# A Mamba scan on VectorE: the product with C one unit late, its broadcast amid the unit, ScalarE's table visits behind the first decay

## The chip, the cores and the metric

The kernel runs on one core of a Trainium2 chip. The metric is the device time of one execution in microseconds, as the median of several runs. The profile is one execution taken by the hardware profiler. Its engines: PE is TensorE (PEld its weight loads), DVE is VectorE, ACT is ScalarE, POOL is GpSimd, SP is SyncE, which only issues DMAs here.

## What is computed

The reference is a hybrid block on an input of 4 x 1024 x 128 floats. Cut to what matters:

```python
x = x + attention(layernorm(x))     # sparse attention, 16 heads
x = x + ffn(layernorm(x))           # 128 -> 512 -> 512 -> 128 with +-1 weights
x = x + mamba(layernorm(x))
x = x + ffn(layernorm(x))           # the same FFN again
return x

# inside mamba: 256 channels e, 16 states n, one step for each time t
def step(h, inp):
    dt_t, B_t, C_t, u_t = inp
    dA = jnp.exp(dt_t[..., None] * A)                       # the decay
    h = dA * h + (dt_t * u_t)[..., None] * B_t[:, None, :]
    y_t = jnp.einsum('ben,bn->be', h, C_t)
    return (h, y_t)
# then y = (y + u * D) * silu(z), a projection back to 128, and the residual
```

## The kernel before, in words

The attention comes first, then set-up and the first FFN tiles; the change does not touch these. Then follows the scan stage (`scans`, called at line 1437), in which everything else still to do of both FFNs and of the Mamba layer is woven between the scans. Behind it stands a tail: whatever pieces of FFN work are left, and the last tiles.

**Units.** A part is one batch element b and one half f of the sequence (512 steps); there are 8 parts. A unit is one state n of one part, so there are 128 units (line 915). The 256 channels lie as two halves h of 128 partitions. For unit i:

- ScalarE makes the decays `da(i,0)` and `da(i,1)` by Exp into PSUM (`decay`, line 1178). There are only two PSUM buffers for them, so `da(i+1,0)` can be written only when the scan that reads `da(i,0)` is through.
- GpSimd makes the drive `db(i)` = du x B, two units ahead (`drive`, line 1151; three buffers).
- VectorE runs two scans over 512 steps, `hs(i,0)` and `hs(i,1)` (line 1263); `hs` has two buffers, so unit i+2 overwrites unit i.
- TensorE spreads C over the partitions in one matmul into the one PSUM buffer `pcc` (line 1257), and VectorE multiplies: `hc(i) = hs(i) * pcc` (line 1280). For the states n = 3, 8 and 13 (`BY_GP`) GpSimd does this product instead, from a C that a DMA has spread (`product_by_gp`, line 1170).
- GpSimd issues for every second unit a DMA that adds `hc(k)` to `hc(k+1)` (`gather`, line 1187), and TensorE sums the results over n in PSUM as `pys` (`add` and `total`, lines 1195 to 1214). At the end of a part VectorE multiplies by the gate (`gated`).
- For f = 0 ScalarE copies the last column of `hs` to `carry` (line 1271), from which the second half of the sequence starts.

**Order.** Inside the scan stage every engine executes in the order in which the program is written (`InOrder`, `keep`). Between a unit's own instructions `pieces(until)` (line 1333) issues work from a set of lists: norms, projections, convolutions, FFN tiles. A piece names how long it occupies which engine. The planner keeps its own clock of each engine in `times`, advanced by `spend`; a piece with TensorE work is issued only if it ends by `until` on that clock, and no engine gets more pieces than an allowance (`RATES`) that is refilled at each call. Evictions from PSUM (`evict=True`) go first. Some evictions are lumps: Silu and Softplus, which need another activation table than Exp, so that ScalarE loads a table, runs two activations and loads Exp's table again. `pieces(..., lumps=False)` does not issue those. Three PSUM banks (`SPARE`) are left for pieces. If a part's preparation isn't issued when a unit needs it, `ready` forces pieces out, at once and whatever they cost.

What is left in the lists after the last unit is issued by the loop at line 1440, still with three banks; then the last tile of the FFN follows with eight banks (line 1446).

Of the kernel before, what the change touches and what calls it, by code (L numbers as in the profile page):

```python
# [16 lines left out]
F32 = mybir.dt.float32  # L17
# [5 lines left out]
ALU = mybir.AluOpType  # L23
# [3 lines left out]
P = 128  # L27
# [10 lines left out]
E, N, DC, DR = 256, 16, 4, 8  # L38
NH = E // P
CH = 512  # L40
# [3 lines left out]
def hybrid_kernel(ctx: ExitStack, tc: tile.TileContext, x, Wq, Wk, Wv, Wo, ln_g, ln_b, W_in, conv_w,  # L44
# [17 lines left out]
    ve, te, sc, gp = (InOrder(e) for e in (nc.vector, nc.tensor, nc.scalar, nc.gpsimd))  # L62
# [19 lines left out]
    for bp in range(NP):  # L82
        t = xpool.tile([P, NT, C], F32, tag=f"x{bp}", name=f"x{bp}")
# [1050 lines left out]
    def scans(wide, ready):  # L1134

        bss, css, dbs, das, hss, hs_of = {}, {}, {}, {}, {}, {}
        BY_GP = (3, 8, 13)
        py = {}  # L1140
        last = len(units) - 1

        def load_b(i):

            if i <= last and i % 2 == 0:
                b, f, n = units[i]
                ready(b, f, "b")
                bss[i] = m2.tile([P, 2, CH], F32, name=f"bs{i}", tag="bs", bufs=2)
                nc.sync.dma_start(bss[i], mamba_pre[b, f][5][n : n + 2, :].partition_broadcast(P))

        def drive(i):
            if i <= last:
                b, f, n = units[i]
                ready(b, f, NH - 1)
                dbs[i] = m2.tile([P, NH, CH], F32, name=f"db{i}", tag="db", bufs=3)
                bs = bss[i - n % 2][:, n % 2]
                gp.tensor_tensor(dbs[i], mamba_pre[b, f][3], bs.unsqueeze(1).to_broadcast([P, NH, CH]), ALU.mult)

        def load_c(i):

            if i <= last and by_gp(i):
                b, f, n = units[i]
                ready(b, f, "b")
                css[i] = m1.tile([P, CH], F32, name=f"cs{i}", tag="cs")
                nc.sync.dma_start(css[i], mamba_pre[b, f][5][N + n, :].partition_broadcast(P))

        def by_gp(i):
            return units[i][2] in BY_GP

        def product_by_gp(i):  # L1170

            if i >= 0 and by_gp(i):
                gp.tensor_tensor(
                    hss[i], hs_of.pop(i), css.pop(i).unsqueeze(1).to_broadcast([P, NH, CH]), ALU.mult
                )
                done["hc", i] = spend("gp", 2.38, *after(("hs", i, 1)))

        def decay(i, h):
            if i <= last:
                b, f, n = units[i]  # L1180
                das[i, h] = wide.tile([P, CH], F32, name=f"da{i}_{h}", tag="da", bufs=2)
                sc.activation(das[i, h], mamba_pre[b, f][2][:, h], AF.Exp, scale=a_t[:, h, n : n + 1])

        def alone(k):
            return k > last - 2

        def gather(i):

            k = i - 2
            if k % 2 or not 0 <= k <= last or alone(k):  # L1190
                return False
            gp.dma_start(hss[k + 1], hss[k], accum_op=ALU.add)
            return True

        def add(k, h):

            b, f, n = units[k]
            first = (b, f, h) not in py
            if first:
                py[b, f, h] = wide.tile([P, CH], F32, name=f"pys{b}_{f}{h}", tag=f"pys{h}")  # L1200
                te.matmul(py[b, f, h], skip_d[:, h], mamba_pre[b, f][1][:, h], start=True, stop=False)
            te.matmul(py[b, f, h], ident, hss[k][:, h], start=False, stop=n == N - 1)
            return 2.0 if first else 1.0

        def total(i):

            us = 0.0
            h = i % 2
            k = i - 3 - h
            if 0 <= k <= last and not alone(k):  # L1210
                us += add(k, h)
            if alone(i - 1):
                us += sum(add(i - 1, h) for h in range(NH))
            return us

        def gated(i):

            h = 1 - i % 2
            k = i - 4 - h
            if 0 <= k <= last and units[k][2] == N - 1 and not alone(k):  # L1220
                gate_by(k, h)
                return True
            return False

        def gate_by(k, h):
            b, f, n = units[k]
            gate = mamba_pre[b, f][0]
            ve.tensor_mul(gate[:, h], gate[:, h], py.pop((b, f, h)))
            if h == NH - 1:
                fed.add(("g", b, f))  # L1230


        done = {}

        def after(*keys):
            return [done.get(k, 0.0) for k in keys]

        for i in range(3):
            load_b(i)
        for i in range(2):  # L1240
            drive(i)
            done["db", i] = spend("gp", 2.38)
        for h in range(NH):
            decay(0, h)
            done["da", 0, h] = spend("sc", 0.7)
        for i, (b, f, n) in enumerate(units):
            now[0] = i
            load_b(i + 3)
            product_by_gp(i - 1)
            load_c(i + 3)  # L1250
            drive(i + 2)
            done["db", i + 2] = spend("gp", 2.38, *after(("hs", i - 1, 1)))
            if gather(i):
                spend("gp", 0.9, *after(("hc", i - 1)))
            if not by_gp(i):
                pc = wide.tile([P, CH], F32, name=f"pcc{i}", tag="pcc")
                te.matmul(pc, spread[: 6 * N, n, :], mamba_pre[b, f][4], start=True, stop=True)
                done["pcc", i] = spend("pe", 0.4, *after(("pcc read",)))
            hs = m2.tile([P, NH, CH], F32, name=f"hs{i}", tag="hs")
            db = dbs.pop(i)  # L1260
            for h in range(NH):
                first = carry[b % 2][:, h, n : n + 1] if f else 0.0
                ve.tensor_tensor_scan(hs[:, h], das.pop((i, h)), db[:, h], first, ALU.mult, ALU.add)
                done["hs", i, h] = spend("ve", 1.235 if f else 1.175, *after(("da", i, h), ("db", i)))
            decay(i + 1, 0)
            done["da", i + 1, 0] = spend("sc", 0.67, *after(("hs", i, 0)))

            t = times["ve"]
            pieces(t + 2.5, lumps=False)
            if f == 0:  # L1270
                sc.copy(carry[b % 2][:, :, n : n + 1], hs[:, :, CH - 1 :])
            decay(i + 1, 1)
            done["da", i + 1, 1] = spend("sc", 0.67 if f else 0.86, *after(("hs", i, 1)))
            if gated(i):
                spend("ve", 0.68, *after(("sum", i - 1)))
            hss[i] = m2.tile([P, NH, CH], F32, name=f"hc{i}", tag="hc", bufs=6)
            if by_gp(i):
                hs_of[i] = hs
            else:
                ve.tensor_tensor(hss[i], hs, pc.unsqueeze(1).to_broadcast([P, NH, CH]), ALU.mult)  # L1280
                done["hc", i] = done["pcc read",] = spend("ve", 1.205, *after(("pcc", i)))
            done["sum", i] = spend("pe", total(i))
            t = times["ve"]
            pieces(t + 2.2)
        total(last + 1)
        for h in range(NH):
            gate_by(last, h)
# [6 lines left out]
    def spend(engine, us, *others):  # L1294
        times[engine] = max(times[engine], *others, 0.0) + us
        return times[engine]
# [36 lines left out]
    def pieces(until, lumps=True):  # L1333

        forced = not until
        evictions(lumps, forced)
        for k, rate in RATES.items():
            owed[k] = min(max(owed[k], -2 * rate) + (0 if forced else rate / 2), rate / 2)  # L1340
        left = SPARE - sum(w.held for w in works)

        for w in works[:-2] + sorted(works[-2:], key=lambda w: w.count):

            moved = w in emptied and now[0] < len(units) - 10
            while w.may() and not w.next.evict and w.next.banks <= left:
                if moved and not w.next.same and not (forced and w in emptied):
                    break
                if not (forced or w.next.hurries()):
                    if any(us and owed[k] <= 0 for k, us in w.next.us.items()):  # L1350
                        break
                    if "pe" in w.next.us and ends(w)[0]["pe"] > until:
                        break
                left -= w.next.banks
                issue(w)
                moved = True
            if forced and moved:
                break
# [121 lines left out]
```

## Time and profile before

| what | value |
|---|---|
| runs | 893.15, 897.59, 889.9 us; median 893.15 us |
| the profiled execution's own time | 896.53 us |
| its span, first to last instruction | 894.7 us, mean granted TensorE clock 0.912 |
| before the scan stage | 322.9 us |
| scan stage, first scan's start to last scan's end | 322.9 to 852.0 us: 529.1 us |
| tail behind the last scan | 42.6 us |
| busy in the scan stage | DVE 474.2, POOL 466.4, PE 458.6, ACT 405.5 us |

The page lists for each group of instructions its busy time and the mean duration of one, then the idle time of its engine just before them and what ended most of it. A line such as `A <- B` among the waits says that A's engine sat idle until B was done. All instructions that go through the ordering helper bear its line, L57, so the names of tiles tell them apart: `hs<-da,db` are scans of first halves, `hs<-da,carry,db` those of second halves.

### The profile page before, as it was taken

The page shows a single profiled execution, that of the slowest core. Times are in us where ns is not written, and L with a number is a line of the kernel's source. Part 1 is how long each engine was busy: PE and PEld are TensorE (multiplying, and loading weights), DVE is VectorE, ACT ScalarE, POOL GpSimd, SP SyncE. Part 2 cuts the span into 40 slices and gives each one's busy share as a digit, 9 for nine tenths or more (in the row PEclk, how much of TensorE's full clock was granted, in tenths as well). Part 3 has the DMA queues.
Part 4 walks back from the last instruction along what each step waited for, and adds up shares of the span by engine and source line. Part 5 has one row for each costly group of instructions (what it writes and reads, how often), then busy time and mean ns, then how long its engine had stood idle before and what let it go on. Part 6 is the DMA issues. An engine that isn't in the chain of part 4 may idle for free. (4 is left out here: it accounts for less than half of the span.)

```text
span 894.7 us, 16435 instructions
## 1 busy us (share of the span) xinstructions
PE 757.9 (85%) x6204; PEld 465.8 (52%) x6204; DVE 726.9 (81%) x970; ACT 606.3 (68%) x1358; POOL 682.5 (76%) x525
## 2 busy tenths in 40 slices
PE   5798878966788977788989788989889689889898
PEld 2455546645667653334546554535545345656567
DVE  6699998999563258898899998898988779999942
ACT  3776656754364488887878778878967766664523
POOL 6689966999342079999989998979979879877800
PEclk9899989997679989797999999899989799999999
DMA  4743133330010036564564656555565545666410
GB/s 127 129 74 73 27 57 68 74 70 2 3 48 1 1 109 155 127 159 129 137 148 130 153 130 153 145 121 138 155 154 133 141 112 150 164 145 153 108 25 19
DMA packets 59808, 92.77 MB, mean 104 GB/s; under 512 B 6200, under 2 KB 39776, under 8 KB 59728
## 3 DMA queue, kind: packets, MB, share of 16 engines
q1 hardware_dynamic: 49488, 58.15, 22.6%
q0 software_dynamic: 9680, 33.30, 19.8%
q8 instruction: 49, 0.80, 0.4%
q10 hardware_dynamic: 560, 0.26, 0.1%
q14 instruction: 31, 0.25, 0.1%
HBM read 52.11 MB, written 4.72 MB: 64 GB/s over the span
## 5 line engine op out<-in xcount | busy, mean ns | idle before, releaser
L57 POOL TENSOR_TENSOR db<-du,bs 128x1024 f32<-128x1024 f32 x128 | 315.6, 2504 | 23.8 <-DVE hs L57 20.1
L57 ACT ACTIVATE da<-dt,a_t 128x512 f32<-128x512 f32 x256 | 175.2, 687 | 107.1 <-DVE hs L57 106.8
L57 DVE TENSOR_TENSOR_SCAN hs<-da,db 128x512 f32<-128x512 f32 x128 | 149.9, 1209 | 29.7 <-ACT da L57 29.5
L57 DVE TENSOR_TENSOR_SCAN hs<-da,carry,db 128x512 f32<-128x512 f32 x128 | 156.7, 1266 | 5.5 <-ACT da L57 5.2
L57 PE MATMUL pys<-hc,ident 128*128 128x512 f32 x258 | 145.3, 649 | 1.9 <-DMA hc<-hc 1.8
L57 DVE TENSOR_TENSOR hc<-hs,pcc 128x1024 f32<-128x1024 f32 x104 | 126.7, 1218 | 22.1 <-PE pcc L57 15.9
L57 POOL TENSOR_TENSOR prodv<-vS,E 128x128 f32<-128x128 f32 (+14 forms) x30 | 69.6, 2319 | 12.2 <-ACT E L57 11.9
L57 PE MATMUL pga<-h1a,w 128*128 128x512 f32 x256 | 72.4, 435 | 5.1 <-ACT u L57 2.9
L57 PEld LDWEIGHTS pys<-hc,ident 128*128 128x128 f32 x258 | 49.6, 208 | 43.6 <-issue 37.2
L57 POOL TENSOR_TENSOR prod<-kv,qs 128x128 f32<-128x128 f32 (+14 forms) x30 | 71.3, 2376 | 1.0 <-DVE or L57 1.0
L57 POOL TENSOR_TENSOR hc<-hs,cs 128x1024 f32<-128x1024 f32 x24 | 58.1, 2421 | 13.6 <-DVE hs L57 11.6
L57 PE MATMUL pc<-mxnT,w_conv 128*128 128x512 f32 x128 | 63.3, 624 | 4.3 <-DVE h1b L57 2.4
L57 PEld LDWEIGHTS pga<-h1a,w 128*128 128x128 f32 x256 | 51.2, 201 | 27.4 <-issue 4.3
L57 POOL DMA_DIRECT2D hc<-hc x63 | 62.7, 995 | 1.8 <-issue 0.9
L57 ACT ACT_TABLE_LOAD x48 | 61.6, 1283 | 3.5 <-issue 2.6
L57 PE MATMUL pcc<-bc,spread 96*128 96x512 bf16 x104 | 42.0, 404 | 22.5 <-DVE hc L57 21.7
L57 ACT ACTIVATE E<-S 128x512 f32<-128x512 f32 (+15 forms) x62 | 26.5, 472 | 38.8 <-DVE S L57 38.6
L57 PE MATMUL ps<-kx,qT 64*32 64x256 f32 x1008 | 46.2, 432 | 6.3 <-DVE S L57 5.0
L57 POOL TENSOR_TENSOR du<-dt,u 128x512 f32<-128x512 f32 x16 | 24.8, 1551 | 29.7 <-ACT dt L57 29.6
L57 PEld LDWEIGHTS pc<-mxnT,w_conv 128*128 128x128 f32 x128 | 25.2, 199 | 37.4 <-issue 31.9
L57 ACT COPY ep<-pt 128x512 f32<-128x512 f32 x32 | 18.8, 587 | 36.4 <-DVE eo L57 36.1
L57 PE MATMUL pgb<-h1b,w 128*128 128x512 f32 x128 | 38.0, 447 | 1.4 <-ACT u L57 1.4
(245 smaller groups left out, 1682.9 us busy)
## 6 DMA issues: line engine op xcount, KB each, us to landing
bs<-bd SPq DMA_DIRECT2D x64, 512.0 KB
hc<-hc POOLq DMA_DIRECT2D x63, 512.0 KB, 4.6
vr<-vd SPq DMA_DIRECT2D x32, 256.0 KB
cs<-bd SPq DMA_DIRECT2D x24, 256.0 KB
vd<-kv SPq DMA_DIRECT2D x8, 256.0 KB
x<-in_L_attn_a_x_dram SPq DMA_DIRECT2D x15, 128.0 KB
kx<-kT SPq DMA_DIRECT2D x104, 16.0 KB
out_dram<-x SPq DMA_DIRECT2D x8, 128.0 KB
```

Source lines behind the costliest of these rows:

```text
L57: ins = getattr(self.engine, name)(*args, **kwargs)
```

## The change

For a unit i, VectorE's order was: scan(i,0), scan(i,1), pieces, gate if one is due, product(i), pieces. It becomes: scan(i,0), product(i-1), pieces, scan(i,1), gate, pieces. The matmul that spreads C for unit i moves from the head of unit i to behind product(i-1) and the first lot of pieces. The decay for (i+1,1) is issued directly behind scan(i,1), ahead of the copy to `carry`. The lumps go into the first lot, so that on ScalarE they stand between `da(i+1,0)` and `da(i+1,1)`; before, they stood between `da(i+1,1)` and `da(i+2,0)`. The DMA that gathers is issued behind product(i-1) of the same unit. The planner's limits change from 2.5 and 2.2 to 1.5 and 2.0 us, and its durations of a scan and a product are each some hundredths lower.

```diff
+        def product(i):
+            if i < 0 or by_gp(i):
+                return
+            hss[i] = m2.tile([P, NH, CH], F32, name=f"hc{i}", tag="hc", bufs=6)
+            ve.tensor_tensor(
+                hss[i], hs_of.pop(i), pcs.pop(i).unsqueeze(1).to_broadcast([P, NH, CH]), ALU.mult
+            )
+            done["hc", i] = done["pcc read",] = spend("ve", 1.15, *after(("pcc", i)))
+
         for i, (b, f, n) in enumerate(units):
...
             done["db", i + 2] = spend("gp", 2.38, *after(("hs", i - 1, 1)))
+            hs = hs_of[i] = m2.tile([P, NH, CH], F32, name=f"hs{i}", tag="hs")
+            db = dbs.pop(i)
+
+            def scan(h):
+                first = carry[b % 2][:, h, n : n + 1] if f else 0.0
+                ve.tensor_tensor_scan(hs[:, h], das.pop((i, h)), db[:, h], first, ALU.mult, ALU.add)
+                done["hs", i, h] = spend("ve", 1.21 if f else 1.15, *after(("da", i, h), ("db", i)))
+                decay(i + 1, h)
+
+            scan(0)
+            done["da", i + 1, 0] = spend("sc", 0.67, *after(("hs", i, 0)))
+            product(i - 1)
             if gather(i):
                 spend("gp", 0.9, *after(("hc", i - 1)))
+            t = times["ve"]
+            pieces(t + 1.5)
             if not by_gp(i):
-                pc = wide.tile([P, CH], F32, name=f"pcc{i}", tag="pcc")
-                te.matmul(pc, spread[: 6 * N, n, :], mamba_pre[b, f][4], start=True, stop=True)
+                pcs[i] = wide.tile([P, CH], F32, name=f"pcc{i}", tag="pcc")
+                te.matmul(pcs[i], spread[: 6 * N, n, :], mamba_pre[b, f][4], start=True, stop=True)
                 done["pcc", i] = spend("pe", 0.4, *after(("pcc read",)))
-            hs = m2.tile([P, NH, CH], F32, name=f"hs{i}", tag="hs")
-            db = dbs.pop(i)
-            for h in range(NH):
-                first = carry[b % 2][:, h, n : n + 1] if f else 0.0
-                ve.tensor_tensor_scan(hs[:, h], das.pop((i, h)), db[:, h], first, ALU.mult, ALU.add)
-                done["hs", i, h] = spend("ve", 1.235 if f else 1.175, *after(("da", i, h), ("db", i)))
-            decay(i + 1, 0)
-            done["da", i + 1, 0] = spend("sc", 0.67, *after(("hs", i, 0)))
-
-            t = times["ve"]
-            pieces(t + 2.5, lumps=False)
+            scan(1)
             if f == 0:
                 sc.copy(carry[b % 2][:, :, n : n + 1], hs[:, :, CH - 1 :])
-            decay(i + 1, 1)
             done["da", i + 1, 1] = spend("sc", 0.67 if f else 0.86, *after(("hs", i, 1)))
             if gated(i):
                 spend("ve", 0.68, *after(("sum", i - 1)))
-            hss[i] = m2.tile([P, NH, CH], F32, name=f"hc{i}", tag="hc", bufs=6)
             if by_gp(i):
-                hs_of[i] = hs
-            else:
-                ve.tensor_tensor(hss[i], hs, pc.unsqueeze(1).to_broadcast([P, NH, CH]), ALU.mult)
-                done["hc", i] = done["pcc read",] = spend("ve", 1.205, *after(("pcc", i)))
+                hss[i] = m2.tile([P, NH, CH], F32, name=f"hc{i}", tag="hc", bufs=6)
             done["sum", i] = spend("pe", total(i))
             t = times["ve"]
-            pieces(t + 2.2)
+            pieces(t + 2.0, lumps=False)
+        product(last)
         total(last + 1)
```

More of the change, by code (lines that the diff above doesn't have):

```diff
@@ L1134, in scans @@
     def scans(wide, ready):
-        bss, css, dbs, das, hss, hs_of = {}, {}, {}, {}, {}, {}
+        bss, css, dbs, das, hss, hs_of, pcs = {}, {}, {}, {}, {}, {}, {}
         BY_GP = (3, 8, 13)
```

## The prediction, made before the changed kernel had run

> **What bounds the kernel now.** I read the page first (shares, slices, groups), then VectorE's waits, then the timelines where they lie; last, since a planner places the pieces, the instruction order of both built programs.
>
> ```profile
> PE 757.9 (85%) x6204; PEld 465.8 (52%) x6204; DVE 726.9 (81%) x970; ACT 606.3 (68%) x1358; POOL 682.5 (76%) x525
> DVE  6699998999563258898899998898988779999942
> ```
> ```profile
> L57 DVE TENSOR_TENSOR_SCAN hs<-da,carry,db 128x512 f32<-128x512 f32 x128 | 156.7, 1266 | 5.5 <-ACT da L57 5.2
> L57 DVE TENSOR_TENSOR hc<-hs,pcc 128x1024 f32<-128x1024 f32 x104 | 126.7, 1218 | 22.1 <-PE pcc L57 15.9
> L57 ACT ACT_TABLE_LOAD x48 | 61.6, 1283 | 3.5 <-issue 2.6
> ```
> ```profile
> DVE hs L57 <- ACT da L57: 34.7, 26, 8.3
> DVE hc L57 <- PE pcc L57: 15.9, 11, 4.3
> ```
>
> In the scan stage (322.9 to 852.0 us, 529.1 us) VectorE is busy 474 us and is the bound: the slices read 8 and 9. It waits 47.9 us there: 26.3 for decays (34.7 less 8.3 before the first scan), 15.9 for spread C, 5.7 for evictions and a gate. So 481.2 us are its own pace. The waits for decays sit behind ScalarE's table visits; one of them:
>
> ```profile
> 618.90 0.69 ACT L57 ACTIVATE da<-dt,a_t 128x512 f32<-128x512 f32 x1
> 619.61 1.28 ACT L57 ACT_TABLE_LOAD   x1
> 620.90 1.27 ACT L57 ACTIVATE dt<-pd,bdt 128x512 f32<-128x512 f32 x2
> 622.19 1.28 ACT L57 ACT_TABLE_LOAD   x1
> 623.48 0.69 ACT L57 ACTIVATE da<-dt,a_t 128x512 f32<-128x512 f32 x1
> ```
> ```profile
> 618.86 1.22 DVE L57 TENSOR_TENSOR hc<-hs,pcc 128x1024 f32<-128x1024 f32 x1
> 620.00 2.33 DVE L57 TENSOR_TENSOR_SCAN hs<-da,db 128x512 f32<-128x512 f32 x2
> 624.27 2.34 DVE L57 TENSOR_TENSOR_SCAN hs<-da,db 128x512 f32<-128x512 f32 x2 [1.95 <-ACT da L57]
> ```
>
> From the scan that frees the first decay's buffer (ended about 618.8) to the scan that needs the second, ScalarE takes 5.4 us: two decays of 0.69, a visit of 3.9, hand-overs. VectorE has 3.6 us of work in that window, and waits the rest.
>
> **The change, part by part** (against the profiled execution: 896.53 us, span 894.7 and 1.8 around it, 3.4 above the median of 893.15).
>
> *The product leaves its own scan.* From start to start in VectorE's timeline a scan with a carry takes 1.19 us ahead of something that doesn't read it and 1.35 ahead of its own product; without a carry 1.13 and 1.29: 0.155 us for the dependence. By the order of before, 73 of 104 products stand straight behind their scan: 73 x 0.155 = -11.3 us. The Trainium skill (VectorE: DVE Perf Modes, The DRAIN you can't avoid) says that the next operation starts only once the pipe is empty, wait or no wait. That speaks against a gain; by it this term is 0 and the forecast 11.3 us longer. The starts above show one, and I take the row.
>
> *Table visits behind the first decay.* I put each of the 22 visits through the same sum: ScalarE's durations between the two decays, VectorE's between the two scans, from the instruction order. As a test on before: 19.6 us at visits and 5.9 elsewhere, 25.5 in all, where the trace has 26.3. For after, ScalarE needs 5.43 as before. VectorE's cover is product, scan, scan, product = 1.14 + 1.16 + 1.16 + 1.14 = 4.60 (before 4.91: two dependences more): 0.83 of wait, at 10 visits. Beside a GpSimd unit one product is missing: 3.46, so 1.97, at 5; with a gate in its place 4.04, so 1.39, at 3. Two are covered (0.17 and 0). At units 62 and 94 a Softplus visit is now forced out when the drive needs it, behind the second decay with only 2.33 and 2.92 us of cover: 4.88 and 2.70. Sum 8.3 + 9.9 + 4.2 + 0.2 + 7.6 = 30.1. Other ScalarE pieces ahead of a second decay beside a GpSimd unit (four normalizations, twice with two sums) give 1.27, 0.14, 1.88, 1.92, 0.43, 1.27, 0.35 = 7.3. So 37.4 for 26.3: +11.1. Bounds: 27 (as before) and 45 (the forced visits doubled). The same skill (ScalarE: Activation LUTs, What ACT_TABLE_LOAD costs) adds a drain of about 1.38 us to each load; above, the next activation starts 0.01 us after it. By the page each visit would be 2.8 us longer, in both versions.
>
> *GpSimd's products lose a product's length of cover.* With two scan buffers, unit i+2's first scan waits for GpSimd's product of unit i. Between them VectorE had two scans, a product, and often a dependence more; now the product lies one scan later, so 1.29 us (1.14 + 0.155) go. In the timelines of before, 7 of 24 such products end within 1.29 us of that scan, for example 0.04 us here (the scans start at 496.57):
>
> ```profile
> 494.17 2.36 POOL L57 TENSOR_TENSOR hc<-hs,cs 128x1024 f32<-128x1024 f32 x1
> ```
>
> Together they lack 7.1 us; some lie beside a visit's wait already, so +5, bounds 1 and 31 (all 24 of them 1.29). GpSimd's drives are hidden: they end 4 to 7 us before their scans.
>
> *Spread C, gather, pys.* The matmul goes behind up to 1.5 us of pieces, not 2.2, and the product asks for it one scan later than its bank is free, as before. TensorE also has less in the stage (below). 9 for 15.9: -6.9; bounds 4 and 20. The gather's DMA is held by the product one scan longer on GpSimd's queue, where the next drive stands behind it; those 4 to 7 us hide that. If a transfer (4.6 us to land) is late for pys, TensorE stalls and the next spread C with it; that is in the upper bound. SP's loads are not moved past anything. The carry copy behind the decay: 0, nothing ended on it.
>
> *Work left over.* With shorter limits fewer pieces fit. Behind the last pys TensorE has 205 matmuls in the order of before and 337 in that of after: the same ones, moved out. In before they ran between 797 and 855 us:
>
> ```profile
> L57 PE MATMUL pgc<-h1c,w 128*128 128x512 f32 x64 | 17.6, 418 | 0.7 <-DVE h1c L57 0.5 <-ACT h2c L57 0.2
> L57 PE MATMUL pfoc<-w,h2c 128*128 128x128 f32 x64 | 8.3, 278 | 0.0
> L57 PE MATMUL pfc<-fxnTc,w 128*128 128x512 f32 x8 | 3.0, 481 | 0.8 <-ACT h2c L57 0.8
> ```
>
> With pmo (2.7 + 1.7), the 256-wide pfc (2.6) and ftpc (1.2) that is 37.1 us. The tail has no room for it:
>
> ```profile
> 857.60:876.30 18.70, 17.44 (x136) 15.27 (x136) 4.68 (x17) 6.08 (x17) 1.26 (x2) 1.00 0.03 9
> 876.30:894.60 18.30, 13.94 (x117) 13.50 (x116) 4.95 (x13) 5.93 (x18) 0.00 (x0) 0.97 0.07 22
> ```
>
> TensorE is busy 17.4 of 18.7 us with three banks, and the last 18.3 us are the last tile's own chain, which waits for the FFN in front of it. So +37; bounds 28 (the 5.7 idle us filled and a clock of 1.00 instead of 0.92) and 45 (evictions with three banks exposed). VectorE's share of that work leaves the stage: six h1c, two ox, four statistics, two narrow fxnTc: -7.1.
>
> *Sum.* Stage: -11.3 + 11.1 + 5 - 6.9 - 7.1 = -9.2. Tail +37. Together +27.8: 924.3 against the profiled 896.5, and 921 against the median.
>
> **The rivals.**
>
> 1. *The visits hide after all.* The second decay's scan now stands behind a scan and two products; if ScalarE gets far enough ahead for that to cover a visit, waits on decays go to 0 instead of 37.4: 921 - 37.4 = 883.5, not slower. Against it: 5.43 of ScalarE does not fit in 4.60, and the same sum meets the trace of before within 1 us. It decides from about 10 us of such waits: below that the kernel gains, above it loses.
> 2. *The tail is cheap.* Moved matmuls fill its gaps (+28), and waits in the stage stay at 47.9 in all: 481.2 - 11.3 - 7.1 + 47.9 = 510.7, -18.4; 893.15 - 18.4 + 28 = 903. For it: TensorE is idle 5.7 us there, less work crowds the stage. Against it: the last 18.3 us wait for that work.
> 3. *GpSimd's products set the pace.* If all 24 come late, 31 instead of 5: 947. For it: POOL is busy 466 of 529 us. Against it: its drives stand 4 to 7 us ahead, and waits of VectorE give it time.
>
> **How the numbers follow.** Forecast 0.62 (912 to 936), rival 1 0.07 (876 to 896), rival 2 0.15 (897 to 911), rival 3 0.16 (936 to 955). The time is the forecast's, 921. The range 898 to 947 leaves out rival 1 and half of rival 3. A measurement here tells about 1% from no change: faster means under 884.2, slower over 902.1. Half of rival 1 is faster: 0.04. The other half and over half of rival 2 are the same: 0.12. The rest is slower: 0.84.
>
> **What would show it.** Right: scans end near 843 us and the tail is 75 to 85 us, TensorE nearly full in it; starts of scan and following product 1.13 to 1.19 apart; second scans (not first ones) of a unit wait for decays, 30 us or more in the stage, worst at units 62 and 94; little wait for spread C. Wrong: a stage under 490 us, waits on decays under 15, or a tail under 65.

## The result, and the profile after

The changed kernel takes 924.88 us (median of 4 runs, 923.36 to 926.06) for 891.74 us before, measured beside it: 1.036 times as long, 95% interval 1.031 to 1.041. The forecast was 921 us, with a range of 898 to 947. The profiled execution took 926.06 us, with a span of 924.2. The two profiles differ by 29.5 us, less than the medians (33.1), because the profiled execution of before, 896.53 us, lies above the median of before.

| part of the span, us | before | after | difference | forecast |
|---|---|---|---|---|
| ahead of the first scan (the same instructions) | 322.9 | 320.8 | -2.1 | 0 |
| scan stage | 529.1 | 523.9 | -5.2 | -9.2 |
| tail | 42.6 | 79.5 | +36.9 | +37 |
| VectorE in the stage: its own pace | 481.2 | 460.9 | -20.3 | -18.4 |
| waits for decays | 26.3 | 28.5 | +2.2 | +11.1 |
| waits for spread C | 15.9 | 17.5 | +1.6 | -6.9 |
| waits for GpSimd | 0 | 13.3 | +13.3 | +5 |
| other waits | 5.7 | 3.8 | -1.9 | 0 |

The stage became 5 us shorter and the tail 37 us longer. Of the waits for GpSimd, 11.6 us are for its products and 1.7 for one drive. From the page of the changed kernel, engines' shares and VectorE's slices:

```profile
PE 752.6 (81%) x6204; PEld 460.9 (50%) x6204; DVE 720.5 (78%) x970; ACT 608.5 (66%) x1358; POOL 683.9 (74%) x525
DVE  6699999999524288797898998788997988997222
```

The work is the same, instruction for instruction, and so are the busy times within 7 us; all shares are lower because the span is longer. VectorE's last three slices read 2 where before only the last one did: the tail is three slices now. The windows of the changed kernel show the stage, the tail with three PSUM banks, and the last tile (columns: stretch, its length, then busy us and instructions of PE, PEld, DVE, ACT, POOL, granted clock, DMA share, GB/s):

```profile
320.80:844.70 523.90, 425.31 (x1465) 229.70 (x1464) 460.50 (x447) 397.65 (x840) 466.28 (x335) 0.93 0.57 140
844.70:905.90 61.20, 56.43 (x328) 44.12 (x326) 15.06 (x41) 16.76 (x40) 2.97 (x6) 0.93 0.04 12
905.90:924.20 18.30, 13.93 (x116) 13.50 (x116) 4.90 (x13) 5.94 (x18) 0.00 (x0) 1.00 0.07 22
```

TensorE is busy 56.4 of 61.2 us in the tail, while VectorE and ScalarE have 15 and 17 us of work there. In the stage TensorE lost 33 us of work (458.6 to 425.3) and that by itself shortened nothing, since VectorE sets the stage's pace. The last tile is the same 18.3 us.

VectorE's waits in the changed kernel (us in all, times, longest):

```profile
DVE hs L57 <- ACT da L57: 28.5, 20, 5.0
DVE hc L57 <- PE pcc L57: 17.5, 13, 4.3
DVE hs L57 <- POOL hc L57: 11.6, 10, 4.1
DVE hs L57 <- POOL db L57: 1.7, 1, 1.7
```

The first two stood in the profile before with 26.3 us in the stage and 15.9; the waits for GpSimd are new.

### The profile page after: what moved, and what is told of

It is laid out like the page before. It is cut to its first block, busy times and chain, and to the rows that moved or that the text cites. A ratio compares the mean times of both kernels' runs of the same rounds, so it can differ in the third digit from the quotient of the medians.

```text
span 924.2 us, 16448 instructions
## 1 busy us (share of the span) xinstructions
PE 752.6 (81%) x6204; PEld 460.9 (50%) x6204; DVE 720.5 (78%) x970; ACT 608.5 (66%) x1358; POOL 683.9 (74%) x525
## 5 line engine op out<-in xcount | busy, mean ns | idle before, releaser
L57 POOL TENSOR_TENSOR db<-du,bs 128x1024 f32<-128x1024 f32 x128 | 318.9, 2540 | 17.7 <-DVE hs L57 10.8
L57 DVE TENSOR_TENSOR_SCAN hs<-da,carry,db 128x512 f32<-128x512 f32 x128 | 158.7, 1268 | 17.1 <-ACT da L57 11.4
L57 PE MATMUL pys<-hc,ident 128*128 128x512 f32 x258 | 147.9, 661 | 7.0 <-DMA hc<-hc 7.0
L57 DVE TENSOR_TENSOR hc<-hs,pcc 128x1024 f32<-128x1024 f32 x104 | 124.5, 1197 | 17.5 <-PE pcc L57 17.5
L57 PEld LDWEIGHTS pys<-hc,ident 128*128 128x128 f32 x258 | 51.7, 207 | 85.2 <-issue 55.2
L57 PE MATMUL pcc<-bc,spread 96*128 96x512 bf16 x104 | 42.6, 410 | 43.6 <-DVE hc L57 43.5
L57 POOL TENSOR_TENSOR prodv<-vS,E 128x128 f32<-128x128 f32 (+14 forms) x30 | 69.6, 2319 | 11.6 <-ACT E L57 11.4
L57 POOL TENSOR_TENSOR hc<-hs,cs 128x1024 f32<-128x1024 f32 x24 | 59.6, 2484 | 16.8 <-DVE hs L57 12.9
L57 PEld LDWEIGHTS pga<-h1a,w 128*128 128x128 f32 x256 | 50.4, 200 | 28.5 <-issue 5.3
L57 PE MATMUL pc<-mxnT,w_conv 128*128 128x512 f32 x128 | 59.5, 598 | 0.8 <-DVE h1b L57 0.8
L57 POOL TENSOR_TENSOR du<-dt,u 128x512 f32<-128x512 f32 x16 | 21.2, 1395 | 31.8 <-ACT dt L57 31.8
```

The costliest lines, as they stand in the source:

```text
L57: ins = getattr(self.engine, name)(*args, **kwargs)
```

## The experiments

The theory: the changed order and the planner's shorter limits together leave TensorE work over that the tail pays in full, while in the stage VectorE gains the time that it lost to the dependence (the product had to wait for its own scan) and gives as much back, 13.3 us, to a new wait for GpSimd. The rivals: the new order as such fills the stage, so that work put back would lengthen it as much; or the limits alone are to blame; or the place of the table visits. TensorE's matmuls behind the last pys are counted from the instruction order of each kernel; the traces show more records there (252 where the count is 205, 432 where it is 337).

**e1, the limits of before in the new order.**

```diff
-            pieces(t + 1.5)
+            pieces(t + 2.5)
...
-            pieces(t + 2.0, lumps=False)
+            pieces(t + 2.2, lumps=False)
```

> The changed kernel with the planner's two limits of before (2.5 and 2.2 us in place of 1.5 and 2.0), all else as changed. Behind the last pys TensorE has 257 matmuls (changed kernel 337, before 205). The two measured tails, 42.6 us at 205 and 79.5 at 337, give 0.28 us a matmul. Theory (the loss is FFN work left over for the tail): tail 57 us, 22 less; the stage takes back VectorE's share, some 4 us; about 907 us. Rival (the new order itself makes the stage full, and work put back lengthens it by as much): 922 to 927 us, with a stage of about 545 us for 523.9.

Measured: 913.17 us, 1.025 of before (1.020 to 1.029), between the two. The tail fell even further than the theory says, to 51.9 us, but the stage grew by 16.8 us to 540.7, nearer the rival's 545 than the theory's 528. VectorE's own pace rose by 6.1 us to 467.0, and its three main waits rose too:

```profile
DVE hs L57 <- ACT da L57: 32.4, 17, 16.6
DVE hc L57 <- PE pcc L57: 20.5, 16, 3.0
DVE hs L57 <- POOL hc L57: 16.6, 10, 3.5
```

A single wait for a decay stands out, in VectorE's timeline of this kernel:

```profile
572.63 3.63 DVE L57 TENSOR_TENSOR_SCAN hs<-da,carry,db 128x512 f32<-128x512 f32 x3
592.84 1.28 DVE L57 TENSOR_TENSOR_SCAN hs<-da,carry,db 128x512 f32<-128x512 f32 x1 [16.58 <-ACT da L57]
```

That is the first scan of unit 63. In unit 62 the next part's preparation had not been issued in time and was forced out between two decays; in the changed kernel the same scan waited 4.98 us. It waits 11.6 us longer here, but the other waits for decays became 7.7 us shorter, so this one wait doesn't explain the longer stage. Taken alone, e1 leaves the rival open.

**e2, limits and allowances both wider.** Limits 3.0 and 3.0, and:

```diff
-    RATES = {"pe": 2.9, "ve": 1.2, "sc": 2.4, "gp": 1.2}
+    RATES = {"pe": 3.2, "ve": 1.3, "sc": 2.6, "gp": 1.3}
```

> The changed kernel with both limits at 3.0 us and allowances raised from 2.9, 1.2, 2.4, 1.2 to 3.2, 1.3, 2.6, 1.3. 181 matmuls are left behind the last pys. Theory (left-over work): tail about 36 us, 43 less than the changed kernel's 79.5; stage longer by VectorE's share and some more waits for spread C, 8 us; about 890 us, level with before. Rival (the stage is full): about 922 to 927 us.

Measured: 892.84 us, 1.002 of before (0.999 to 1.005). Windows of this kernel:

```profile
318.80:854.30 535.50, 461.60 (x1671) 261.90 (x1670) 469.96 (x468) 407.61 (x866) 467.56 (x339) 0.91 0.55 138
854.30:892.30 38.00, 33.59 (x239) 28.19 (x237) 10.81 (x30) 10.97 (x32) 1.26 (x2) 0.95 0.07 19
```

TensorE has 461.6 us of work in the stage again, 36 more than in the changed kernel, and the stage is 11.6 us longer while the tail is 41.5 us shorter. So the stage was not full. The theory holds, and with it goes the whole loss: the new order, given enough pieces, is level with the kernel before. Whether the limits or the allowances did it was not separated. The stage itself gained nothing: it is 6.4 us longer than before, the tail 4.6 us shorter and the stretch ahead of the stage, with the same instructions, 4.1 us shorter.

**e3, the limits and planned durations alone, in the old order.**

```diff
-            pieces(t + 2.5, lumps=False)
+            pieces(t + 1.5, lumps=False)
...
-            pieces(t + 2.2)
+            pieces(t + 2.0)
```

and the planned durations 1.21, 1.15 and 1.15 of the changed kernel.

> The kernel before, in its own order, with the changed kernel's limits (1.5 and 2.0 us) and planned durations (scan 1.21 and 1.15, product 1.15). 223 matmuls are left behind the last pys, for 205. Theory (limits and order together leave the work over; limits alone do little): tail 5 us longer, stage up to 5 us shorter: 888 to 898 us. Rival (limits and durations alone make the loss): 915 us or more.

Measured: 891.23 us, 1.001 (0.998 to 1.004); tail 45.4 us. In the old order the limits do nothing. Matmuls left over: 205 before; 223 with the limits and planned durations alone, 257 with the order and those durations (e1), 337 with all. The two work on each other.

**e4, the table visits alone behind the first decay, in the old order.**

```diff
-            pieces(t + 2.5, lumps=False)
+            pieces(t + 2.5)
...
-            pieces(t + 2.2)
+            pieces(t + 2.2, lumps=False)
```

> The kernel before, with the table visits alone moved behind the first decay (lumps in the first lot of pieces, not in the second); product still straight after its own scan. Theory (what covers a visit is the work of VectorE between the two scans around it): in this order the cover is scan, product, scan = 3.6 us against 5.4 of ScalarE; the sum over all windows gives 51 us of waits for decays for 25.5 in before; 189 matmuls are left, so the tail is 4 us shorter: about 913 us. Rival (the place of the visits hardly matters, ScalarE catches up elsewhere): 886 to 896 us.

Measured: 909.35 us, 1.020 (1.015 to 1.024). VectorE's wait for decays in this kernel, the start of the stage (8.3 us) included:

```profile
DVE hs L57 <- ACT da L57: 50.0, 26, 8.3
```

41.7 us within the stage, for 26.3 before. The window sum had 51, so it was too high; the time is near the 913 expected, and the rival is out.

**e5, the visits alone put back behind the second decay, in the new order.** The same exchange, in the changed kernel.

> The changed kernel with the table visits back where they were (lumps in the second lot of pieces), all else as changed. 337 matmuls are left behind the last pys, as in the changed kernel. Theory (a visit is covered by what VectorE has between the two scans around it): behind the second decay the cover is now scan, product, scan = 3.5 us for 5.4; the window sum gives some 50 us of waits for decays where the changed kernel measured 28.5; tail the same: 938 to 946 us. Rival (the place of the visits doesn't matter): 922 to 927 us.

Measured: 936.19 us, 1.048 of before (1.044 to 1.052), where the changed kernel has 1.036. That is just under the theory's range and well over the rival's.

```profile
DVE hs L57 <- ACT da L57: 43.2, 21, 7.6
```

43.2 us for 28.5. So a visit's place and the product's place belong together: 26.3 (both old), 41.7 (visits moved alone), 43.2 (product moved alone), 28.5 (both moved; these last two with the shorter limits). The move of the visits doesn't lower the waits; it keeps the product's move from raising them.

**e6, three buffers for the scans' results.** In exchange the buffers that hold the products go from six to five, at all three places that name them; one is shown.

```diff
-            hs = hs_of[i] = m2.tile([P, NH, CH], F32, name=f"hs{i}", tag="hs")
+            hs = hs_of[i] = m2.tile([P, NH, CH], F32, name=f"hs{i}", tag="hs", bufs=3)
...
-            hss[i] = m2.tile([P, NH, CH], F32, name=f"hc{i}", tag="hc", bufs=6)
+            hss[i] = m2.tile([P, NH, CH], F32, name=f"hc{i}", tag="hc", bufs=5)
```

> The changed kernel with three buffers for the scans' results (hs) and five for the products (hc), for two and six; same order of instructions. Theory (the new wait for GpSimd's products, 11.6 us, is a wait for the scan buffer): it vanishes, the stage is 8 to 11 us shorter, the tail stays at 79 us: 914 to 917 us. Rival (VectorE then waits at the next thing, GpSimd's drives or decays): 921 to 926 us.

Measured: 920.61 us, 1.031 (1.027 to 1.034). The wait for GpSimd's products is gone, so it was a wait for the buffer; but the stage is only 3.2 us shorter (520.7). VectorE's waits in this kernel:

```profile
DVE hs L57 <- ACT da L57: 31.3, 21, 5.0
DVE hc L57 <- PE pcc L57: 17.6, 11, 3.9
DVE hs L57 <- POOL db L57: 3.5, 2, 1.8
```

Beside 11.6 us less there are 2.8 more for decays, 1.8 more for drives and 3.4 more for evictions and a gate, 8.0 in all. So the time comes nearer the rival's than the theory's: some 70% of the wait moved on.

**e7, e2 with the third buffer.**

> The changed kernel with limits of 3.0 us, allowances of 3.2, 1.3, 2.6, 1.3 and three scan buffers (five for products): both losses that the theory names undone. Against the same without the third buffer (892.8 us, waits for GpSimd's products 10.6 us): theory 882 to 885 us, 1% under before. Rival (the wait moves on): 890 to 894 us.

Measured: 886.23 us, 0.992 of before (0.989 to 0.996). The lowest median of the study, just above the theory's 882 to 885, and below that of both kernels. Its profiled execution, one of the faster ones (span 879.3), has a stage of 524.7 and a tail of 36.4 us. Here the buffer's wait did not move on:

```profile
DVE hc L57 <- PE pcc L57: 22.9, 19, 3.4
DVE hs L57 <- ACT da L57: 21.3, 22, 2.7
```

Waits for GpSimd are 2.8 us for 11.3 in e2, for decays 21.3 for 19.2, for spread C 22.9 for 24.6.

**e8, the allowances of e2 alone, in the old order.**

> The kernel before in its own order and limits, with the allowances alone raised to 3.2, 1.3, 2.6, 1.3. 189 matmuls are left behind the last pys, for 205. It says what the allowances give without the new order. Theory (the new order is worth its 11 us of dependence and pays for it with waits for GpSimd and for spread C): tail 4 us shorter, window sum of waits for decays 18.6 for 25.5: 880 to 887 us. Rival (the raised allowances only help the new order): 889 to 894 us.

Measured: 889.04 us, 0.995 (0.994 to 0.997): the rival's number more than the theory's. VectorE's waits in this kernel (8.3 us of the first are the start of the stage):

```profile
DVE hs L57 <- ACT da L57: 24.6, 23, 8.3
DVE hc L57 <- PE pcc L57: 15.2, 14, 2.6
DVE hs L57 <- POOL hc L57: 3.0, 3, 1.6
```

So it has waits for decays of 16.3 us for 26.3, but a tail of 44.0 us, no shorter than before. Against e2, with the same allowances and nearly the same work in the stage (468 instructions of VectorE in both), it shows what the order does, though e2's limits are wider as well: VectorE's own pace 482.6 us here, 471.1 in e2, so 11.5 us less; waits for spread C and GpSimd 19.0 here, 36.0 in e2. The order's gain is real and is eaten by these two: at like allowances the new order is the slower one (1.002 of before in e2, 0.995 here, and the intervals do not meet). Between e7 and e8 the intervals overlap, so which of them is the faster stays open, and no gain by the new order over the old one is shown.

**e9, the spread of C at the head, in the changed kernel.** The matmul goes ahead of the first lot of pieces.

```diff
-            t = times["ve"]
-            pieces(t + 1.5)
             if not by_gp(i):
...
+            t = times["ve"]
+            pieces(t + 1.5)
             scan(1)
```

> The changed kernel with the matmul that spreads C ahead of the first lot of pieces, straight behind the product that frees its bank, all else as changed. The planner then counts TensorE as taken up to the product's end before each first lot, and 493 matmuls are left behind the last pys (changed kernel 337). Theory (what is left over is paid for in the tail at 0.28 us a matmul): tail about 123 us; the window sum gives up to 60 us of waits for decays, for 28.5 measured; waits for spread C fall from 17.5 to under 10: 960 to 990 us. Rival (the tail is cheap beyond some point, since TensorE runs undisturbed there): 930 to 950 us.

Measured: 1025.26 us, 1.148 (1.144 to 1.152), well over both expectations. The tail is 110.9 us for 493 matmuls (0.24 us each over before's 205, not 0.28), and waits for spread C are 0.85 us, as expected. What neither theory had is the stage, 594.4 us, with 89.1 us of waits for decays within it and 37.5 of evictions that waited for FFN matmuls. VectorE's timeline of this kernel:

```profile
575.52 0.75 DVE L57 SCALAR_TENSOR_TENSOR x<-pfoa,total,x 128x512 f32<-128x512 f32 x1 [15.27 <-PE pfoa L57]
...
603.92 2.46 DVE L57 TENSOR_TENSOR_SCAN hs<-da,carry,db 128x512 f32<-128x512 f32 x2 [24.16 <-ACT da L57]
```

With so few pieces placed, the preparation of the parts at units 64 and 96 was forced out whole. The longest single wait, 36.5 us, stands at unit 94. So this run says little of the matmul's place by itself.

**e10, the spread at the head, in e7, with limits of 4.0.**

> The version of limits 3.0, raised allowances and three scan buffers (886.2 us, tail 36.4, waits for spread C 22.9 us), with the matmul that spreads C ahead of the first lot and limits of 4.0 us, so that 215 matmuls are left for 181. Theory (the matmul's wait is its place behind up to 3 us of pieces on TensorE's queue): waits for spread C fall to about 10, tail 9 us longer: 880 to 885 us. Rival (the product waits for TensorE wherever the matmul stands, since the bank is free only for two scans): 890 to 896 us.

Measured: 897.58 us, 1.006 (1.004 to 1.008): 12 us over the theory's range and even over the rival's. VectorE's waits in this kernel (8.3 us of the first are the start of the stage):

```profile
DVE hs L57 <- ACT da L57: 49.3, 36, 8.3
DVE hc L57 <- PE pcc L57: 5.0, 6, 1.8
```

The wait for spread C falls from 22.9 to 5.0 us: it does come from the matmul's place behind pieces on TensorE's queue, and there the theory's mechanism holds. The tail is 45.3 us, 9 more, as expected. But waits for decays rise from 21.3 to 41.0 within the stage, more than the 17.9 us that were saved. Whether that is the longer lots that a limit of 4.0 allows on ScalarE or the earlier matmul was not told apart.

## Why the prediction was right, point by point

*The work left over* carried it: +37 forecast, +36.9 measured. It was read without any time of the new kernel: the instruction order says which matmuls move behind the last pys, the trace of before what they took there. That it agrees to 0.1 us is luck: TensorE's busy time in the tail rose by 33.4 us (37.0 to 70.4), not 37.1, and its idle time by 3.5 (5.6 to 9.1), where the step left it as it was. All runs together, in order of the matmuls left over:

| matmuls left | tail, us |
|---|---|
| 181 | 38.1 (e2), 36.4 (e7) |
| 189 | 41.8 (e4), 44.0 (e8) |
| 205 | 42.6 (before) |
| 215 | 45.3 (e10) |
| 223 | 45.4 (e3) |
| 257 | 51.9 (e1) |
| 337 | 79.5 (changed kernel), 77.4 (e5), 79.2 (e6) |
| 493 | 110.9 (e9) |

The tail follows the count, at no fixed price: 0.18 us a matmul from 205 to 257, 0.35 from there to 337 and 0.20 from there to 493.

*The product leaves its own scan*: right in kind and size. VectorE's own pace fell by 20.3 us for 18.4 forecast (11.3 of dependence and 7.1 of moved work), and e2 against e8 gives 11.5 us for the order. Both differences also hold something that was not forecast: each of the 104 products became 0.026 us shorter (last section), some 2.7 us by our estimate. In the timeline of the changed kernel:

```profile
745.68 2.45 DVE L57 TENSOR_TENSOR_SCAN hs<-da,carry,db 128x512 f32<-128x512 f32 x2
748.05 1.19 DVE L57 TENSOR_TENSOR hc<-hs,pcc 128x1024 f32<-128x1024 f32 x1
749.16 2.45 DVE L57 TENSOR_TENSOR_SCAN hs<-da,carry,db 128x512 f32<-128x512 f32 x2
```

Two scans and a product go by in 3.48 us. In the timeline before, where the product follows its own scan:

```profile
771.47 2.45 DVE L57 TENSOR_TENSOR_SCAN hs<-da,carry,db 128x512 f32<-128x512 f32 x2
774.01 1.22 DVE L57 TENSOR_TENSOR hc<-hs,pcc 128x1024 f32<-128x1024 f32 x1
775.15 2.45 DVE L57 TENSOR_TENSOR_SCAN hs<-da,carry,db 128x512 f32<-128x512 f32 x2
```

it takes 3.68. The second scan of each pair starts 1.19 us behind the first and takes 1.26. In the changed kernel the product, which belongs to another unit, starts 1.18 us after that scan's start, 0.08 us before the profile has it end; before, the scan's own product started 1.35 us after it, 0.09 us behind its end.

The prediction weighed a rule of the Trainium skill (VectorE: DVE Perf Modes, The DRAIN you can't avoid), that the next operation starts only when the pipe is empty, whether or not it waits, and read from it a gain of 0. That reading was too narrow: the same section adds that a next operation that is not held starts earlier. The rows above show such a start, and the gain with it.

*Table visits*: the mechanism was right, the sum too large. Forecast 37.4 us of waits for decays, measured 28.5. At single visits the window sum is good: for the one forced out in unit 62, 4.88 forecast and 4.98 measured (at the first scan of unit 63); in 94, 2.70 and 2.70 (unit 95); at the second scans of units 7, 0.83 and 0.87, and 25, 1.97 and 1.99. Unit 62 on ScalarE in the changed kernel:

```profile
583.06 1.07 ACT L57 ACTIVATE h2a<-pga 128x512 f32<-128x512 f32 x2
584.14 1.28 ACT L57 ACT_TABLE_LOAD   x1
585.44 1.27 ACT L57 ACTIVATE dt<-pd,bdt 128x512 f32<-128x512 f32 x2
586.72 1.28 ACT L57 ACT_TABLE_LOAD   x1
588.02 1.30 ACT L57 ACTIVATE da<-dt,a_t 128x512 f32<-128x512 f32 x2
```

and on VectorE, the wait that it makes:

```profile
580.21 3.62 DVE L57 TENSOR_TENSOR_SCAN hs<-da,carry,db 128x512 f32<-128x512 f32 x3
588.81 1.28 DVE L57 TENSOR_TENSOR_SCAN hs<-da,carry,db 128x512 f32<-128x512 f32 x1 [4.98 <-ACT da L57]
```

The 22 visits made 23.1 us for 30.1 forecast, other places 5.4 for 7.3. What failed is adding the terms up. At units 15, 28, 58 and 107 the sum had 5.6 us of wait for decays and there is none, because in the same windows VectorE already waited 4.1 us for GpSimd, 4.3, 1.7 and 1.9 for spread C. In these four windows the two waits did not add up. The other 3.3 us of the 8.9 were not traced to a place.

*Spread C*: wrong in sign. Forecast 9, measured 17.5. The step held that less TensorE work in the stage and a shorter lot ahead of the matmul would bring it earlier. In the middle it does: half of these matmuls start within 0.80 us of the bank coming free, for 1.18 before, and TensorE waits longer for the bank, 43.5 us for 21.7. But VectorE waits only for the late ones, 13 of them for 11 before, and these are no earlier than then. (Two scans, some 2.4 us, pass between the bank coming free and the next product, in both orders, not one as the step has it.) The longest, 4.30 us, from TensorE's timeline of the changed kernel:

```profile
432.78 1.03 PE L57 MATMUL pfa<-fxnTa,w 128*128 128x512 f32 x2
436.47 1.12 PE L57 MATMUL pfa<-fxnTa,w 128*128 128x512 f32 x2 [2.66 <-ACT gate L57]
437.39 3.21 PE L57 MATMUL pfoa<-w,h2a 128*128 128x128 f32 x16
440.43 0.38 PE L57 MATMUL pcc<-bc,spread 96*128 96x512 bf16 x1
```

The spread stands behind a piece that itself waits for ScalarE, and behind another of 3.2 us. e10 has more TensorE work in the stage than the changed kernel (451.7 us for 425.3) but the matmul ahead of the pieces, and waits 5.0 us: it is the pieces in front of it in TensorE's order, not the total. e5, with the table visits elsewhere and the same work left over, has 11.4 us; why was not traced.

*GpSimd's products*: the named mechanism (two scan buffers, a product's length less cover), but 11.6 us for 5, within the bounds of 1 and 31. Another 1.7 us went to a drive, which the step called hidden because the drives end 4 to 7 us before their scans; in the trace of before that holds for the middle half, 27 of the 128 end less than 4 us ahead, and in the changed kernel half end less than 3.5 us ahead. The worst wait for a product, from GpSimd's timeline of the changed kernel:

```profile
375.60 2.76 POOL L57 TENSOR_TENSOR du<-dt,u 128x512 f32<-128x512 f32 x2
378.05 2.60 POOL L57 TENSOR_TENSOR db<-du,bs 128x1024 f32<-128x1024 f32 x1
380.36 2.60 POOL L57 TENSOR_TENSOR hc<-hs,cs 128x1024 f32<-128x1024 f32 x1
```

and VectorE's:

```profile
383.00 1.22 DVE L57 TENSOR_TENSOR_SCAN hs<-da,db 128x512 f32<-128x512 f32 x1 [4.10 <-POOL hc L57]
```

The product of unit 13 could have begun when its second scan ended at 376.6, but it stood behind two du and a drive in GpSimd's queue. The term was taken from the lateness in the trace of before, and lateness changes when other work moves. e6 confirms the buffer.

The errors of these three terms, -8.9 (decays), +8.5 (spread C) and +8.3 (GpSimd, drive included), partly cancel: the stage's forecast is within 4 us by luck as much as by sizing. Of the signs named beforehand, the scans' end (844.7 us), the tail, the full TensorE in it and the short step from scan to product came; waits for decays fell just short of the 30 us named, and 9.9 of their 28.5 us are at first scans, most of it from the two forced visits; little wait for spread C did not come. The rivals: the visits did not hide; the cheap tail did not come; GpSimd's products set the pace at ten units, not at 24.

## What to carry to other kernels

When a planner places filler work between a kernel's own instructions, look first at where the filler ends up: here the work that no longer fitted the stage was paid for behind it, on an engine that had little cover there. Count it from the instruction order and price it with the trace of before. A reorder that shortens the bound engine's pace may need its limits, allowances and buffers widened in the same step: here the order with its shorter limits lost 3.6%, and with wider limits, raised allowances and one buffer more it stood 0.8% under the kernel before. Then test the widening without the reorder: the raised allowances alone, in the old order, gave 0.5%, and the intervals overlap. Waits estimated window by window were good one by one, but could not be added where two of them shared a window.

## What the runs showed of the hardware that was not expected

The product itself, start to start, takes 1.112 us in the changed kernel where it took 1.138 before (median of those directly followed by a scan), apart from the dependence. It is 1.112 or 1.113 in every run of the new order and 1.138 in every run of the old one. GpSimd's product and drive are a little slower in the changed kernel, 2484 and 2540 ns for 2421 and 2504 on average. No run isolates a cause of either.

The granted clock over the stage is 0.92 before, 0.93 in the changed kernel and 0.82 in e9, where TensorE stood 99.9 us at the spread matmul waiting for the product. That these waits lower it is not shown: e10 has 51.1 us of them at 0.92, and e5 34.7 us at 0.87.
